# A mixture-of-experts layer on one Trainium2 core: expert results added to totals in memory instead of stored by slot and gathered by token

## The chip, the core and the metric

The kernel runs on one core of one Trainium2 chip. The metric is the device time of the whole program in microseconds (us), lower is better. The engines are named as the profile names them: PE (TensorE, matrix multiply), DVE (VectorE), ACT (ScalarE), POOL (GpSimd) and SP (SyncE). SP and POOL also issue the transfers (DMAs): SP the plain ones for inputs, weights and outputs, POOL those of this change, among them the ones whose rows are chosen by a list of indices.

## What is computed

512 tokens (8 sequences of 64) of 512 numbers each pass through three residual layers: attention to a context of 8 x 1601 rows, a graph-like attention among the 64 tokens of a sequence, and a mixture of 8 experts. The change is in the third, so the rest is left out here:

```python
logits = x @ router_w.T + router_b                     # 8 logits a token
topk_val, topk_idx = jax.lax.top_k(logits, 2)
weights = jax.nn.softmax(topk_val, axis=-1)            # two weights a token
h = xf @ wa.T + ba                                     # an expert: 512 -> 2 x 2048
h1, h2 = jnp.split(h, 2, axis=-1)
out = (silu(h1) * h2) @ wb.T + bb                      # -> 512
combined = (gathered * weights.reshape(-1, 2, 1)).sum(axis=1)
x = x + combined
```

`gathered` holds, for each token, the outputs of its two experts. All arithmetic is in float32.

## The kernel before

**The front, 0 to 385 us.** Tokens are handled in four tiles of 128, held in `xs[t]`. Generators for the steps of a tile (`queries`, `scores`, `average`, `mix`, `attend`, `route`) are interleaved by a hand-made clock, and TensorE's order is pinned with explicit dependencies (`in_line`). After the first tile's `average`, `clear` writes zeros to the DRAM tensor `sorted_x` (8 x 512 rows of 512 numbers), after the second's to `sorted_y` of the same size.

**Routing.** `route(t)` normalizes a tile into `xr`, computes logits, picks two experts for each token and counts, for each expert, how many earlier tokens chose it. That gives each token two places, `expert * 512 + position`, kept in `place`, and two weights, kept in `weight`. Two indirect DMAs on POOL (L583) scatter the rows of `xr` to these places of `sorted_x`. The experts' output bias, weighted, is added to `xs[t]` at once (L603), so that `xs[t]` is what the experts' outputs are still to be added to.

**The experts, 385 to 880 us.** The number of tokens of each expert is loaded into registers of PE, ACT, DVE and POOL. Each expert's rows are handled in blocks of up to 128, by `level(e, j, xT)`: where at most 64 rows of a block are left, the arm `narrow` runs, otherwise `dense`, and after a dense block, where more than 128 rows are left, the next level. All arms exist in the program; every engine branches for itself. An arm that an engine doesn't take has instructions of its own, which make up for the semaphore counts of the arm.

- `dense` takes transposed rows `xT`. For each of 16 chunks of the hidden layer it computes `h` (L769, a PSUM tile with two buffers), ACT applies silu (L777), DVE adds the bias and multiplies (L780). It then transposes the next block's rows (`turn`, L740) and accumulates the output `o` over the 16 chunks (L791). ACT copies `o` to `y` (L795) and POOL stores `y` to `sorted_y` (L796).
- `narrow` holds 64 rows, with the two halves of the 128 partitions working on different columns. Four steps of matmuls (L812, L824), silu (L832), a multiply on DVE (L833), transposes (L836) and a copy (L837) give the hidden layer; `on` is accumulated (L843), copied by ACT (L851) and stored in two pieces (L854).
- Rows are loaded from `sorted_x` by `load_rows_of` (L725) on POOL, with dependencies on all eight scatters. The first block of an expert is loaded two experts ahead, a further block at the start of the dense block before it.
- Weights come in panels of 1 MB over SP (L153), 12 for each expert.

With this input the blocks are, from the trace: expert 0 dense; 1 and 2 narrow; 3 and 4 dense; 5 narrow; 6 three dense and one narrow; 7 dense and narrow. That is 7 dense and 5 narrow blocks.

**The end.** For each tile and each of a token's two places an indirect DMA on POOL gathers rows of `sorted_y` (L909), DVE multiplies by the weight and adds to `xs[t]` (L915), and SP stores the tile (L918).

Of the kernel before, what the change touches and what calls it, by code (L numbers as in the profile page):

```python
# [9 lines left out]
F32 = mybir.dt.float32  # L10
AF = mybir.ActivationFunctionType
ALU = mybir.AluOpType
AX = mybir.AxisListType
PSUM = bass.MemoryType.PSUM

P = 128
# [4 lines left out]
def tile_perceiver_layer(  # L21
# [27 lines left out]
    nc = tc.nc  # L49
    B, T, D = x.shape  # L50
    S = context.shape[1]
    NT = B * T
    NTT = NT // P
# [3 lines left out]
    E = b2.shape[0]  # L57
# [7 lines left out]
    outf = out.flatten_outer_dims()  # L65

    const = ctx.enter_context(tc.tile_pool(name="const", bufs=1))
    small = ctx.enter_context(tc.tile_pool(name="small", bufs=2))
# [7 lines left out]
    xs = [const.tile([P, D], F32, name=f"xs{t}") for t in range(NTT)]  # L76
# [37 lines left out]
    for e in range(1, E):  # L114
# [7 lines left out]
        out=tri, in_=tri, pattern=[[1, P]], compare_op=ALU.is_gt, fill=0.0, base=0,  # L122
        channel_multiplier=-1,
# [6 lines left out]
        nc.gpsimd.memset(first[:, e : e + 1], float(e * NT))  # L130
    masks = const.tile([P, NTT, E], F32, name="masks")
    place = const.tile([P, NTT, 2], mybir.dt.int32, name="place")
    weight = const.tile([P, NTT, 2], F32, name="weight")
    counts = const.tile([1, E], mybir.dt.int32, name="counts")
    scatters = []

    dram = ctx.enter_context(tc.tile_pool(name="dram", bufs=1, space=bass.MemoryType.DRAM))
    sorted_x = dram.tile([E * NT, D], F32, name="sorted_x")  # L140
    sorted_y = dram.tile([E * NT, D], F32, name="sorted_y")


    NPAN = NP1 + NP2
# [11 lines left out]
    def layernorm(dst, src):  # L156
        mean, rstd = moments(src)
        nc.vector.tensor_scalar(dst, src, mean, rstd, ALU.subtract, ALU.mult)
# [14 lines left out]
    with ExitStack() as attn:  # L173
# [49 lines left out]
        def buffers(t):  # L223
            return wide if t < NTT - 1 or not cross_done else beside[0]

        def pair(t):
            return 2 if buffers(t) is wide else 1
# [39 lines left out]
        qks, qbs = {}, {}  # L267

        def queries(t):
            xn = wide.tile([P, D], F32, tag="xr", name="xn", bufs=2)  # L270
            layernorm(xn, xs[t])
            hT = turned(t, xn)
            yield 0.8
            qT = wide.tile([P, ND, P], F32, tag="vT", name="qT")
            add_bias(qT, project_T(t, wq_sb, hT), bq_sb)
            yield 0.8
            qks[t] = tok.tile([P, ND, P], F32, tag="qk", name="qk", bufs=NTT)
            nc.vector.tensor_copy(qks[t], project_T(t, wk_sb, qT))
            qb_ps = bank(t, [P, 1], "few", "qb_ps")
            for k in range(ND):  # L280
                matmul(qb_ps, qT[:, k, :], bk_sb[:, k : k + 1], start=(k == 0), stop=(k == ND - 1))
            qbs[t] = small.tile([P, 1], F32, tag="qb", name="qb", bufs=NTT)
            nc.vector.tensor_scalar(qbs[t], qb_ps, SCALE, None, ALU.mult)
# [134 lines left out]

        avgs = {}

        def clear(rows_of, avg):

            zeros = wide.tile([P, D], F32, tag="y", name="zeros")
            nc.vector.tensor_tensor(zeros, avg, avg, ALU.is_lt)
            for e in range(E):
                nc.gpsimd.dma_start(
                    out=rows_of[e * NT : (e + 1) * NT, :].rearrange("(j p) d -> p j d", p=P),
                    in_=zeros.unsqueeze(1).to_broadcast([P, NTT, D]),
                )

        def mix(t):

# [91 lines left out]


        def route(t):
            xn = buffers(t).tile([P, D], F32, tag="xr", name="xr", bufs=pair(t))
            layernorm(xn, xs[t])
            yield 7.5
            rT = turned(t, xn)  # L530
            yield 1.0
# [22 lines left out]
            for u in range(t + 1):  # L554
# [13 lines left out]
            nc.vector.reciprocal(norm, norm)  # L568
            nc.vector.tensor_scalar(told[:, 1, :], told[:, 1, :], norm, None, ALU.mult)
            nc.vector.tensor_tensor(told[:, 0, :], pos, first, ALU.add)  # L570
            both = small.tile([P, 2, 2, E], F32, tag="both", name="both", bufs=2)
            nc.vector.tensor_tensor(
                both,
                picks.unsqueeze(2).to_broadcast([P, 2, 2, E]),
                told.unsqueeze(1).to_broadcast([P, 2, 2, E]),
                ALU.mult,
            )
            found = small.tile([P, 2, 2], F32, tag="found", name="found")
            nc.vector.tensor_reduce(found, both, AX.X, ALU.add)
            nc.vector.tensor_copy(place[:, t, :], found[:, :, 0])  # L580
            nc.vector.tensor_copy(weight[:, t, :], found[:, :, 1])
            for c in range(2):
                scatter = nc.gpsimd.indirect_dma_start(  # L583
                    out=sorted_x,
                    out_offset=bass.IndirectOffsetOnAxis(ap=place[:, t, c : c + 1], axis=0),
                    in_=xn,
                    in_offset=None,
                )

                for other in scatters:  # L590
                    tc.declare_no_dep(scatter.ins, other.ins, reason="no two tokens share a row")
                scatters.append(scatter)
# [8 lines left out]
            mm = bank(t, [P, D], "", "mm")  # L601
            matmul(mm, gT, b2_sb, start=True, stop=True)
            nc.vector.tensor_tensor(xs[t], mm, xs[t], ALU.add)  # L603

        def hidden_bias_rows():
            for i in range(b1.shape[1] // P):
# [36 lines left out]
        def crossing(first):  # L643

            for t in range(NTT):
                yield from first if t == 0 else scores(t, 1)
                yield from average(t)
                averaged.append(t)
                if t < 2:
                    clear([sorted_x, sorted_y][t], avgs[t])  # L650
                for j in range(1, NSB):
                    if t + 1 < NTT:
                        load_context(t + 1, j)
                if t + 2 < NTT:
                    load_context(t + 2, 0)
            cross.close()
            early.append(ctx.enter_context(tc.tile_pool(name="early", bufs=EARLY, side="right")))
            beside.append(attn.enter_context(tc.tile_pool(name="beside", bufs=1, side="right")))
            cross_done.append(True)
            for n in range(EARLY):  # L660
                load_panel(n)
            probs.append(clear_probs(beside[0]))
# [46 lines left out]
    with ExitStack() as ffn:  # L709
# [9 lines left out]
        NC2 = NC1 // NP2  # L719
        NB = NT // P  # L720
        engines = [mybir.EngineType.PE, mybir.EngineType.Activation, mybir.EngineType.DVE, mybir.EngineType.Pool]
        def load_rows_of(e, j):
            r = rows.tile([P, D], F32, tag="r", name="r")
            at = e * NT + j * P
            read = nc.gpsimd.dma_start(out=r, in_=sorted_x[at : at + P, :])  # L725
            for scatter in scatters:
                tc.add_manual_dep(
                    read.ins,
                    scatter.ins.name,
                    mybir.DependencyInfo(  # L730
                        mybir.DependencyClass.Sync, mybir.DependencyReason.DATA
                    ),
                    reason="rows of any tile",
                )
            return r

        def turn(r, tag, after=None):
            tr = banks.tile([P, ND, P], F32, tag="t" + tag[0] + tag[-1], name="t")
# [19 lines left out]
        def dense(e, j, xT):  # L758

            r = load_rows_of(e, j + 1) if j + 1 < NB else None  # L760
            g = gpool.tile([P, NC1, P], F32, tag="g", name="g", bufs=1)
            for n in range(NC1):
                w = panels[e * NPAN + n // PC].rearrange(
# [28 lines left out]
                    o, g[:, n, :], w2_chunk(e, n), start=(n == 0), stop=(n == NC1 - 1)  # L792
                )
            y = gpool.tile([P, D], F32, tag="y", name="y")
            nc.scalar.copy(y, o)  # L795
            nc.gpsimd.dma_start(out=sorted_y[e * NT + j * P : e * NT + (j + 1) * P, :], in_=y)  # L796
            return ahead

        def narrow(e, j, xT):


            s = P // 2
            G = P // s
            M = NP1 // G
            W = D // G
            gT = gpool.tile([P, M, PC, P], F32, tag="gT", name="gT", bufs=1)
            for m in range(M):
                h = banks.tile([P, 2, PC, P], F32, tag="hn", name="hn", bufs=2)
# [39 lines left out]
                        stop=(n == NC1 - 1),  # L848
                    )
            y = gpool.tile([P, W], F32, tag="yn", name="yn")  # L850
            nc.scalar.copy(y, o)  # L851
            at = e * NT + j * P
            for q in range(G):
                nc.gpsimd.dma_start(  # L854
                    out=sorted_y[at : at + s, q * W : (q + 1) * W], in_=y[q * s : (q + 1) * s, :]
                )

# [43 lines left out]
            tc.no_sync_barrier()  # L903
            level(e, 0, turned_rows[e])

        for t in range(NTT):
            for c in range(2):
                y = rows.tile([P, D], F32, tag="r", name="back")
                nc.gpsimd.indirect_dma_start(  # L909
                    out=y,  # L910
                    out_offset=None,
                    in_=sorted_y,
                    in_offset=bass.IndirectOffsetOnAxis(ap=place[:, t, c : c + 1], axis=0),
                )
                nc.vector.scalar_tensor_tensor(  # L915
                    xs[t], y, weight[:, t, c : c + 1], xs[t], ALU.mult, ALU.add
                )
            nc.sync.dma_start(out=outf[t * P : (t + 1) * P, :], in_=xs[t])  # L918


# [65 lines left out]
```

## Time and profile before

| what | before |
|---|---|
| median of 3 runs | 905.05 us (903.5 to 906.7) |
| the profiled execution | 905.28 us, span 903.5 us |
| PE busy | 771.2 us (85% of the span) |
| DVE, ACT, POOL busy | 225.9, 159.6, 66.9 us |
| mean clock granted to TensorE | 0.932 |
| bytes moved by DMA | 165.99 MB |
| `sorted_x` clears, issue to landing | 19.1 us median of 8, 1 MB each |
| scatters to `sorted_x` | 3.4 us median of 8 |
| loads of rows `r` | 6.6 us median of 15, 256 KB each |
| stores of `y`; of `yn` | 6.8 us (7 of 256 KB); 5.4 us (10 of 64 KB) |
| gathers from `sorted_y` | 4.0 us median of 8 |

A row of the order of time reads: start and duration in us, engine, line, operation, what is written and what is read, how many were merged, and in brackets the engine's idle time before it and what ended it. Registers, branches, semaphores and the issue of a DMA are not counted as busy. A releaser is inferred: where the one named had long been done, it was another. Times of a DMA are from its issue to its landing.

### The profile page before, as it was taken

What the parts mean: (1) busy time and instruction counts of PE and PEld (TensorE: products, weight loads), DVE (VectorE), ACT (ScalarE), POOL (GpSimd) and SP (SyncE); (2) the same over time, 40 slices, a digit from 0 to 9 for tenths busy, and PEclk for the clock granted to TensorE, in tenths of its full rate; (3) what the DMA queues carried; (4) which work ended last, traced back from release to release, by engine and by line L of the source; (5) the groups of instructions that cost most, each with busy time, mean ns of one, the idle gap of its engine ahead of it and who ended that gap; (6) DMA issues with size and microseconds to landing.
All of it is one profiled execution on the core that took longest, in us unless ns stands there. A gap on an engine that the chain in (4) does not pass through costs nothing. (4 is left out here: it accounts for less than half of the span.)

```text
span 903.5 us, 11522 instructions
## 1 busy us (share of the span) xinstructions
PE 771.2 (85%) x4794; PEld 517.8 (57%) x4794; DVE 225.9 (25%) x514; ACT 159.6 (18%) x324; POOL 66.9 (7%) x114
## 2 busy tenths in 40 slices
PE   3997997997999874399998896998899999969980
PEld 3883544444454442297454875945878786559450
DVE  2322265255342464111111110201111111101012
ACT  1123144034132123021110111100111110012000
POOL 5100200300000000100000000000000000000003
PEclk9998998999899997589999898999899999979995
DMA  9930970790420821900899957749940000062004
GB/s 304 363 135 1 366 298 0 266 415 7 151 71 1 332 88 57 396 15 2 324 403 417 403 206 302 294 155 419 408 181 24 3 24 1 1 266 93 12 5 142
DMA packets 40315, 165.99 MB, mean 184 GB/s; under 512 B 3552, under 2 KB 3568, under 8 KB 27936
## 3 DMA queue, kind: packets, MB, share of 16 engines
q1 hardware_dynamic: 31968, 136.34, 38.9%
q0 software_dynamic: 8256, 28.42, 8.3%
q8 instruction: 59, 0.97, 0.4%
q14 instruction: 32, 0.26, 0.1%
HBM read 142.34 MB, written 22.41 MB: 182 GB/s over the span
## 5 line engine op out<-in xcount | busy, mean ns | idle before, releaser
L769 PE MATMUL h<-x,panel 128*128 128x128 f32 x1024 | 124.6, 288 | 22.1 <-PEq L868 21.4
L769 PEld LDWEIGHTS h<-x,panel 128*128 128x128 f32 x1024 | 123.4, 204 | 23.9 <-issue 22.6
L780 DVE SCALAR_TENSOR_TENSOR g<-h,b_sb,g 128x128 f32<-128x128 f32 x112 | 39.3, 351 | 232.3 <-ACT g L777 232.3
L791 PE MATMUL o<-panel,g 128*128 128x512 f32 x224 | 97.3, 592 | 0.0
L791 PEld LDWEIGHTS o<-panel,g 128*128 128x128 f32 x224 | 42.1, 190 | 50.2 <-issue 50.2
L777 ACT ACTIVATE g<-h,b_sb 128x128 f32<-128x128 f32 x112 | 41.1, 367 | 150.3 <-PE h L769 150.2
L201 PEld LDWEIGHTS ctr<-ident,c 128*128 128x128 f32 x384 | 43.1, 145 | 40.6 <-DVE cT L333 13.3
L201 PE MATMUL ctr<-ident,c 128*128 128x128 f32 x384 | 54.4, 286 | 13.1 <-DMA c<-in_context_dram 11.5
L769 PEld LDWEIGHTS h<-xT,panel 128*128 128x128 f32 x512 | 57.3, 192 | 2.8 <-issue 2.8
L769 PE MATMUL h<-xT,panel 128*128 128x128 f32 x512 | 57.6, 276 | 1.2 <-ACTq L868 0.6
L205 PE MATMUL sc_ps<-cT,qk 128*64 128x512 f32 (+1 forms) x256 | 54.4, 524 | 4.9 <-ACT sc L326 4.9
L333 DVE COPY cT<-ctr 128x512 f32<-128x512 f32 (+1 forms) x52 | 34.8, 670 | 61.6 <-PE ctr L201 61.2
L812 PE MATMUL hn<-panel,x 128*64 128x512 f32 x192 | 49.3, 605 | 0.0
L331 ACT COPY cT<-ctr 128x512 f32<-128x512 f32 (+1 forms) x52 | 29.6, 570 | 111.2 <-PE ctr L201 111.2
L205 PE MATMUL av<-c,pT 128*64 128x512 f32 x192 | 48.4, 642 | 0.0
L843 PE MATMUL on<-panel,gT 128*64 128x256 f32 x320 | 38.6, 381 | 0.0
L833 DVE TENSOR_TENSOR gn<-hn,gn 128x256 f32<-128x256 f32 x20 | 8.5, 425 | 103.3 <-ACT gn L832 97.7
L205 PEld LDWEIGHTS mm<-hT,w 128*128 128x128 f32 x256 | 29.2, 192 | 8.8 <-DVE hT L237 8.8
L205 PE MATMUL mm<-hT,w 128*128 128x128 f32 x256 | 30.7, 278 | 4.0 <-DVE hT L237 4.0
L812 PE MATMUL hn<-panel,xT 128*64 128x512 f32 x128 | 32.2, 596 | 0.0
L769 PE MATMUL h<-xd,panel 128*128 128x128 f32 x256 | 31.3, 288 | 0.8 <-DVE xd L751 0.8
L843 PEld LDWEIGHTS on<-panel,gT 128*64 128x64 f32 x320 | 24.5, 137 | 12.9 <-issue 0.8
(175 smaller groups left out, 703.2 us busy)
## 6 DMA issues: line engine op xcount, KB each, us to landing
panel<-in_w_dram SPq DMA_DIRECT2D x96, 1024.0 KB, 15.6
c<-in_context_dram SPq DMA_DIRECT2D x24, 1024.0 KB, 10.9
sorted_x<-zeros POOLq DMA_DIRECT2D x8, 1024.0 KB, 19.1
sorted_y<-zeros POOLq DMA_DIRECT2D x8, 1024.0 KB, 18.9
r<-sorted_x POOLq DMA_DIRECT2D x15, 256.0 KB, 6.6
sorted_y<-y POOLq DMA_DIRECT2D x7, 256.0 KB, 6.8
cl<-in_context_dram SPq DMA_DIRECT2D x8, 130.0 KB
xs<-in_x_dram SPq DMA_DIRECT2D x4, 256.0 KB, 8.4
```

Of the source, the lines that this page charges most:

```text
L201: in_line(nc.tensor.transpose(out, in_, identity))
L205: in_line(nc.tensor.matmul(out, lhsT, rhs, **flags))
L331: nc.scalar.copy(dst, tr)
L333: nc.vector.tensor_copy(dst, tr)
L769: last = nc.tensor.matmul(h[:, half, :], w[:, k, half, (n % PC) * P : (n % PC + 1) * P], xT[:, k, :], start=(k == 0), stop=(k == ND - 1),)
L777: nc.scalar.activation(g[:, n, :], h[:, 0, :], AF.Silu, bias=b1_sb[:, col : col + 1])
L780: nc.vector.scalar_tensor_tensor(g[:, n, :], h[:, 1, :], b1_sb[:, col + NC1 : col + NC1 + 1], g[:, n, :], ALU.add, ALU.mult,)
L791: nc.tensor.matmul(o, g[:, n, :], w2_chunk(e, n), start=(n == 0), stop=(n == NC1 - 1))
L812: nc.tensor.matmul(h[q * s : (q + 1) * s].rearrange("p h c d -> p (h c d)"), xT[:, k, :s], w[:, k, :], start=(k == 0), stop=(k == ND - 1),)
L833: nc.vector.tensor_tensor(gn, h[:, 1], gn, ALU.mult)
L843: nc.tensor.matmul(o[q * s : (q + 1) * s, :], gT[:, m, c, i * s : (i + 1) * s], w2_chunk(e, n)[:, q * W : (q + 1) * W], start=(n == 0), st ...
```

## The change

Results no longer go by slot to `sorted_y`. Two tensors of totals in DRAM, one for each half of the 512 columns, take their place.

- Each row of `sorted_x` gets 9 more numbers (521 in place of 512, `WIDE`): the token's number, counted from 1, and its weight for each of the 8 experts (0 where it is not chosen). The token's number is written by POOL, the weights by DVE, into the same tile `row` that is scattered. `clear` zeroes `sorted_x` only, and 128 spare rows at the end of each total.
- After the bias is added, `route` writes `xs[t]` to the totals, in two halves: two more DMAs on POOL for each tile.
- Each block loads its 9 numbers for each row (`load_shares`, on POOL; a narrow block once for each half of the partitions) and turns them on DVE, in three small instructions, into the row of the totals for each partition. An empty slot has the number 0, and is sent to a spare row of its own.
- DVE, not ACT, takes `o` out of PSUM, and multiplies by the weight. Two indirect DMAs that add (`add_to_total`) take the place of the store.
- At the end SP copies the two totals to the output, from DRAM to DRAM. The gathers, the multiply-adds and the stores of the tiles are gone.

The core of the diff:

```diff
-    sorted_x = dram.tile([E * NT, D], F32, name="sorted_x")
-    sorted_y = dram.tile([E * NT, D], F32, name="sorted_y")
+    WIDE = D + 1 + E
+    sorted_x = dram.tile([E * NT, WIDE], F32, name="sorted_x")
+    total = [dram.tile([1 + NT + P, D // 2], F32, name=f"total{h}") for h in range(2)]
...
+            zeros = wide.tile([P, WIDE], F32, tag="xr", name="zeros", bufs=2)
...
+            for h in range(2):
+                nc.gpsimd.dma_start(out=total[h][1 + NT :, :], in_=zeros[:, : D // 2])
...
+            nc.gpsimd.tensor_scalar(row[:, D : D + 1], number, float(t * P), None, ALU.add)
...
-            nc.vector.tensor_copy(weight[:, t, :], found[:, :, 1])
+            nc.vector.tensor_copy(row[:, D + 1 :], told[:, 1, :])
...
             nc.vector.tensor_tensor(xs[t], mm, xs[t], ALU.add)
+            for h in range(2):
+                nc.gpsimd.dma_start(
+                    out=total[h][1 + t * P : 1 + (t + 1) * P, :],
+                    in_=xs[t][:, h * D // 2 : (h + 1) * D // 2],
+                )
...
-                if t < 2:
-                    clear([sorted_x, sorted_y][t], avgs[t])
+                if t == 0:
+                    clear(avgs[t])
...
+        def load_shares(e, j, s):
+            shares = rows.tile([P, 1 + E], F32, tag="shares", name="shares", bufs=2)
+            for q in range(P // s):
+                read_sorted(shares[q * s : (q + 1) * s, :], e * NT + j * P, s, D, WIDE)
+            to = rows.tile([P, 1], mybir.dt.int32, tag="to", name="to", bufs=2)
+            row = rows.tile([P, 1], F32, tag="row", name="row", bufs=2)
+            nc.vector.tensor_scalar(row, shares[:, 0:1], 0.0, beyond, ALU.is_equal, ALU.mult)
+            nc.vector.tensor_tensor(row, row, shares[:, 0:1], ALU.add)
+            nc.vector.tensor_copy(to, row)
+            return to, shares[:, 1 + e : 2 + e]
+
+        def add_to_total(h, y, to):
+            nc.gpsimd.indirect_dma_start(
+                out=total[h],
+                out_offset=bass.IndirectOffsetOnAxis(ap=to, axis=0),
+                in_=y,
+                in_offset=None,
+                compute_op=ALU.add,
+            )
...
             r = load_rows_of(e, j + 1) if j + 1 < NB else None
+            to, weight = load_shares(e, j, P)
             g = gpool.tile([P, NC1, P], F32, tag="g", name="g", bufs=1)
...
-            nc.scalar.copy(y, o)
-            nc.gpsimd.dma_start(out=sorted_y[e * NT + j * P : e * NT + (j + 1) * P, :], in_=y)
+            nc.vector.tensor_scalar(y, o, weight, None, ALU.mult)
+            for h in range(2):
+                add_to_total(h, y[:, h * D // 2 : (h + 1) * D // 2], to)
...
+            to, weight = load_shares(e, j, s)
             gT = gpool.tile([P, M, PC, P], F32, tag="gT", name="gT", bufs=1)
...
-            nc.scalar.copy(y, o)
+            nc.vector.tensor_scalar(y, o, weight, None, ALU.mult)
             for q in range(G):
-                nc.gpsimd.dma_start(
-                    out=sorted_y[at : at + s, q * W : (q + 1) * W], in_=y[q * s : (q + 1) * s, :]
-                )
+                add_to_total(q, y[q * s : (q + 1) * s, :], to[:s])
...
-        for t in range(NTT):
-            for c in range(2):
-                y = rows.tile([P, D], F32, tag="r", name="back")
-                nc.gpsimd.indirect_dma_start(
...
-            nc.sync.dma_start(out=outf[t * P : (t + 1) * P, :], in_=xs[t])
+        for h in range(2):
+            nc.sync.dma_start(out=outf[:, h * D // 2 : (h + 1) * D // 2], in_=total[h][1 : 1 + NT, :])
```

`read_sorted` is the body of the old `load_rows_of`, with the columns as arguments; `load_rows_of` now reads columns 0 to 511 with it.

More of the change, by code (lines that the diff above doesn't have):

```diff
@@ L132, in tile_perceiver_layer @@
     place = const.tile([P, NTT, 2], mybir.dt.int32, name="place")
-    weight = const.tile([P, NTT, 2], F32, name="weight")
     counts = const.tile([1, E], mybir.dt.int32, name="counts")
     scatters = []
+    number = const.tile([P, 1], F32, name="number")
+    nc.gpsimd.iota(
+        number, pattern=[[0, 1]], base=1, channel_multiplier=1, allow_small_or_imprecise_dtypes=True
+    )
+    beyond = const.tile([P, 1], F32, name="beyond")
+    nc.gpsimd.tensor_scalar(beyond, number, float(NT), None, ALU.add)
     dram = ctx.enter_context(tc.tile_pool(name="dram", bufs=1, space=bass.MemoryType.DRAM))
-    sorted_x = dram.tile([E * NT, D], F32, name="sorted_x")
-    sorted_y = dram.tile([E * NT, D], F32, name="sorted_y")
+    WIDE = D + 1 + E
+    sorted_x = dram.tile([E * NT, WIDE], F32, name="sorted_x")
+    total = [dram.tile([1 + NT + P, D // 2], F32, name=f"total{h}") for h in range(2)]
     NPAN = NP1 + NP2
@@ L269, in queries @@
         def queries(t):
-            xn = wide.tile([P, D], F32, tag="xr", name="xn", bufs=2)
+            xn = wide.tile([P, WIDE], F32, tag="xr", name="xn", bufs=2)[:, :D]
             layernorm(xn, xs[t])
@@ L419, in tile_perceiver_layer, with clear @@
         avgs = {}
-        def clear(rows_of, avg):
-            zeros = wide.tile([P, D], F32, tag="y", name="zeros")
-            nc.vector.tensor_tensor(zeros, avg, avg, ALU.is_lt)
+        def clear(avg):
+            zeros = wide.tile([P, WIDE], F32, tag="xr", name="zeros", bufs=2)
+            nc.vector.tensor_tensor(zeros[:, :D], avg, avg, ALU.is_lt)
+            nc.vector.tensor_copy(zeros[:, D:], zeros[:, : 1 + E])
             for e in range(E):
                 nc.gpsimd.dma_start(
-                    out=rows_of[e * NT : (e + 1) * NT, :].rearrange("(j p) d -> p j d", p=P),
-                    in_=zeros.unsqueeze(1).to_broadcast([P, NTT, D]),
-                )
+                    out=sorted_x[e * NT : (e + 1) * NT, :].rearrange("(j p) d -> p j d", p=P),
+                    in_=zeros.unsqueeze(1).to_broadcast([P, NTT, WIDE]),
+                )
+            for h in range(2):
+                nc.gpsimd.dma_start(out=total[h][1 + NT :, :], in_=zeros[:, : D // 2])
         def mix(t):
@@ L526, in route @@
         def route(t):
-            xn = buffers(t).tile([P, D], F32, tag="xr", name="xr", bufs=pair(t))
+            row = buffers(t).tile([P, WIDE], F32, tag="xr", name="xr", bufs=pair(t))
+            xn = row[:, :D]
             layernorm(xn, xs[t])
+            nc.gpsimd.tensor_scalar(row[:, D : D + 1], number, float(t * P), None, ALU.add)
             yield 7.5
@@ L570, in route @@
             nc.vector.tensor_tensor(told[:, 0, :], pos, first, ALU.add)
-            both = small.tile([P, 2, 2, E], F32, tag="both", name="both", bufs=2)
             nc.vector.tensor_tensor(
[L573 to L576, printed above, removed]
-            )
-            found = small.tile([P, 2, 2], F32, tag="found", name="found")
-            nc.vector.tensor_reduce(found, both, AX.X, ALU.add)
-            nc.vector.tensor_copy(place[:, t, :], found[:, :, 0])
-            nc.vector.tensor_copy(weight[:, t, :], found[:, :, 1])
+                picks, picks, told[:, 0, :].unsqueeze(1).to_broadcast([P, 2, E]), ALU.mult
+            )
+            found = small.tile([P, 2], F32, tag="found", name="found")
+            nc.vector.tensor_reduce(found, picks, AX.X, ALU.add)
+            nc.vector.tensor_copy(place[:, t, :], found)
+            nc.vector.tensor_copy(row[:, D + 1 :], told[:, 1, :])
             for c in range(2):
@@ L585, in route @@
                     out_offset=bass.IndirectOffsetOnAxis(ap=place[:, t, c : c + 1], axis=0),
-                    in_=xn,
+                    in_=row,
                     in_offset=None,
@@ L721, in tile_perceiver_layer, with read_sorted @@
         engines = [mybir.EngineType.PE, mybir.EngineType.Activation, mybir.EngineType.DVE, mybir.EngineType.Pool]
[L722 to L725, printed above, removed]
+        def read_sorted(out, at, n, first, end):
+            read = nc.gpsimd.dma_start(out=out, in_=sorted_x[at : at + n, first:end])
             for scatter in scatters:
@@ L734, in load_rows_of @@
                 )
-            return r
+        def load_rows_of(e, j):
+            r = rows.tile([P, D], F32, tag="r", name="r")
+            read_sorted(r, e * NT + j * P, P, 0, D)
+            return r
+        def load_shares(e, j, s):
[15 more added lines that the diff above has]
+                compute_op=ALU.add,
+            )
         def turn(r, tag, after=None):
@@ L850, in narrow @@
             y = gpool.tile([P, W], F32, tag="yn", name="yn")
-            nc.scalar.copy(y, o)
-            at = e * NT + j * P
+            nc.vector.tensor_scalar(y, o, weight, None, ALU.mult)
             for q in range(G):
-                nc.gpsimd.dma_start(
-                    out=sorted_y[at : at + s, q * W : (q + 1) * W], in_=y[q * s : (q + 1) * s, :]
-                )
+                add_to_total(q, y[q * s : (q + 1) * s, :], to[:s])
         def arm(cond, label):
@@ L904, in tile_perceiver_layer @@
             level(e, 0, turned_rows[e])
-        for t in range(NTT):
-            for c in range(2):
-                y = rows.tile([P, D], F32, tag="r", name="back")
[L909 to L917, printed above, removed]
-            nc.sync.dma_start(out=outf[t * P : (t + 1) * P, :], in_=xs[t])
+        for h in range(2):
+            nc.sync.dma_start(out=outf[:, h * D // 2 : (h + 1) * D // 2], in_=total[h][1 : 1 + NT, :])
 def _layout(v):
```

## The prediction

> **What bounds the kernel now.** I read the page first, then busy time and clock by stage, then POOL's order of time in the expert stages with the landing times of its loads, and last the final 25 us. From the page:
>
> ```profile
> span 903.5 us, 11522 instructions
> PE 771.2 (85%) x4794; PEld 517.8 (57%) x4794; DVE 225.9 (25%) x514; ACT 159.6 (18%) x324; POOL 66.9 (7%) x114
> L780 DVE SCALAR_TENSOR_TENSOR g<-h,b_sb,g 128x128 f32<-128x128 f32 x112 | 39.3, 351 | 232.3 <-ACT g L777 232.3
> ```
>
> TensorE (PE) is the bound. VectorE (DVE) has room, but each chunk of a dense block needs one L780 on DVE before its PSUM buffer `h` is free, and `h` has two buffers: DVE costs nothing while on time, and once it is late TensorE stops two chunks later. The order of time of expert 4's dense block, POOL first:
>
> ```profile
> 547.46 0.55 POOL L796 DMA_DIRECT2D sorted_y<-y  x1 [43.06 <-ACTq L868]
> 557.12 0.54 POOL L725 DMA_DIRECT2D r<-sorted_x  x1 [9.11 <-DMA r<-sorted_x]
> 559.17 0.54 POOL L725 DMA_DIRECT2D r<-sorted_x  x1 [1.51 <-DMA r<-sorted_x]
> ...
> 797.53 1.06 POOL L854 DMA_DIRECT2D sorted_y<-yn  x2 [68.34 <-ACTq L873]
> 800.46 0.57 POOL L796 DMA_DIRECT2D sorted_y<-y  x1 [1.87 <-DMA r<-sorted_x]
> ```
>
> ```profile
> 554.12 16.10 PE L769 MATMUL h<-x,panel 128*128 128x128 f32 x120 [6.67 <-PEq L868]
> ```
>
> ```profile
> 562.21 0.37 ACT L777 ACTIVATE g<-h,b_sb 128x128 f32<-128x128 f32 x1 [1.70 <-PE h L769]
> 564.00 0.37 ACT L777 ACTIVATE g<-h,b_sb 128x128 f32<-128x128 f32 x1 [1.42 <-PE h L769]
> ```
>
> POOL is idle 9.11 us between storing expert 3's rows and its next load, since it goes past an arm not taken only when the store has landed (median 6.8 us for L796, 5.4 us for L854). TensorE needs none of that now: rows are loaded a block ahead. But POOL reaches the dense block's own load (559.17) 5 us after TensorE started there. The last two POOL rows show that a queue keeps its order: expert 6's `y` was ready at 769.8 us and stored at 800.46, because another store stood in front, waiting. All loads of rows, issue to landing, in us:
>
> ```profile
> DMA to landing us min/median/max: 2.9/6.6/8.2
> ```
>
> In the two quiet blocks (682 to 735 us, DMA share 0.05) the median is 3.3. A third thing is the clock. After a gap TensorE runs slowly; here expert 4's first 3.9 us, after a gap of 6.67 (columns: PE, weight load, DVE, ACT, POOL busy, then clock, DMA share, GB/s):
>
> ```profile
> 554.10:558.00 3.90, 3.88 (x18) 3.90 (x19) 0.00 (x0) 0.00 (x0) 0.54 (x1) 0.50 1.01 420
> ```
>
> The end, behind the last matmul:
>
> ```profile
> 878.78 0.37 ACT L851 COPY yn<-on 128x256 f32<-128x256 f32 x1 [7.26 <-PE on L843]
> 879.45 1.06 POOL L854 DMA_DIRECT2D sorted_y<-yn  x2 [26.66 <-ACTq L873]
> 884.85 1.01 POOL L909 DMA_INDIRECT back<-sorted_y,place  x1 [4.34 <-issue]
> ...
> 898.40 1.54 DVE L915 SCALAR_TENSOR_TENSOR xs<-back,weight,xs 128x512 f32<-128x512 f32 x2 [0.92 <-DMA back<-sorted_y,place]
> ```
>
> 24 us without a matmul: store, wait, eight gathers, eight multiply-adds, four stores.
>
> **The sum's base.** The profiled execution took 905.28 us (span 903.5, 1.8 around it); the runs' median is 905.05, so the two are taken as one.
>
> **Removed and cheap parts.** The clear of `sorted_y` (eight DMAs, 6.0 us of POOL at 175) goes; in 95 to 215 us TensorE waits for no context load, so this is worth 0. The new rows of totals (eight DMAs of 128 KB and two spare ones, about 0.55 us each on POOL) lie where POOL idles; the last two follow the last token scatters (369.94), and the loads behind them wait 8.03 us for those scatters anyway. If that cover failed: +1.1. Marking and weights in `route` exchange one small DVE instruction for another and add one on POOL: 0. The eviction of `y` moves from ACT (585 ns) to DVE (nearest row: the PSUM copy L751, 690 ns); the next block's first chunks hide it, and at the very end it costs the same as ACT's 0.37.
>
> Rows become 2,084 bytes. No row of the trace has that size; with 2,048 bytes a clear lands in 19.1 us and the slowest token scatter in 8.1. The Trainium skill, "DMA: Bandwidth & Descriptors", section "How a descriptor splits into AXI transactions", splits a row into 256-byte transactions with a leftover and an extra one for an unaligned start: 9 or 10 in place of 8. By the row the change costs 0 at the front; by the rule, estimated, up to a quarter of 8.1 us. I take +1 (0 to +2): the first loads wait for that scatter, TensorE for them. The clear has 35 us of slack before the first scatter.
>
> **The end.** The last block's two adds replace its two stores. By the gathers' rows, 1.0 us each with 0.30 between: the second starts at 880.75. How long an add takes to land no row shows. Bounds: below, the plain store of this place, 1.9; above, twice the slowest token scatter, 16 (each row is read as well as written). I take 4.2, the token scatter's median 3.4 and a little: 885. Passing the arm not taken, as before from 882.0 to 883.6, and the issue: 887. The copy moves 1 MB in two DMAs; nearest rows are an unhindered 1 MB weight load, 5.5 us, and an output store, 2.8: I take 5.5 (2.8 to 11, memory being at both ends). With the 1.5 us that followed the last landing before: 894. So -9 (-4 to -12), were all else equal.
>
> **The new wait.** Every block now loads its tokens and shares (`load_shares`) on POOL and, on DVE, turns them into row numbers at once: three small instructions whose first waits for that load. The block needs the result only at its end, but DVE runs in order, so the L780s or L833s behind them wait too, and with them TensorE. On POOL itself 17 share loads (7 dense blocks, 5 narrow ones with two) and 24 adds stand in place of 17 stores: about 9 + 24 in place of 9 us, spread over 495 us in which it idles; what they delay is POOL's next loads, counted below. SP waits for the adds only with its two copies, and nothing is queued behind those. Where among DVE's instructions the three stand, the trace of before can't show. Bounds: in front of all, or behind so many that the load is in. They come first in the source, but an instruction whose input is not ready can be passed; I take them behind the second chunk or the third of a dense block, and behind the first of a narrow one.
>
> Arrival at expert 4 as the example: POOL at 559.17, later by 1.3 since two adds (1.0 each, 0.3 between) start where one store did and POOL waits for the second; +0.55 to issue the row load that stands in front; +6.6 to land (r's median; the small load follows r's rows on one queue): 567.6; +0.9 for the three (0.16 each) and the L780 behind: 568.5. Behind the second chunk, TensorE can finish the third, and would start the fourth at 562.21: it stops 6.3 us. In the same way, with 3.3 us to land in the quiet blocks and two share loads in a narrow block: expert 3 (503.86, needed 508.9) 4.2; expert 6's three dense blocks (638.87, 685.29, 728.66) 3.6, 3.8, 3.4; expert 7 (806.41, needed 813.7) 2.8. Narrow blocks, needed at the second transpose L836: expert 1 (444.30, needed 448.2) 6.1; expert 2 (474.55, 476.8) 7.6; expert 5 (610.18, 611.9) 8.3. Expert 0 (load issued at 384.62, before TensorE's start), 6's narrow block (POOL idle long before) and 7's last: 0. Sum 46.1. Behind the third chunk each dense block stops 1.8 less: 35.3.
>
> Gaps of 3.8 us and more are followed by the half clock about 4 us after they begin, for 6.8 us (493.4: clock 0.5 from 497.3 to 504.1; 547.4: from 551.9 to 558.7); what of that falls on running matmuls costs half. Five stops are that long: (6.8 - (stop - 4.2))/2 gives 11 us, or 9 in the second case. So 57 or 44; I take 50 between them.
>
> 905.3 + 50 - 9 + 1 = 947.
>
> A rule against that size: the same page, section "Anatomy of one DMA — SWDGE (gpsimd) path", fits 2.0 us plus bytes/436e3 to such a DMA: 2.0 for the 4.6 KB of shares. The row says 6.6 for r beside the panels, 3.3 without. By the rule the stops shrink by 4.6 (1.3) us to 15 in all, none long enough for the half clock, and the sum is 912. The trace's own rows decide: the load shares a queue with r, whose fastest of 15 took 2.9.
>
> **Rivals.** (1) Faster: the three stand so far back that the shares are in. From behind about the eighth dense chunk and the third narrow one, no block stops and only the end counts: 905.3 - 9 + 1 = 897. For it: nothing needs the result early. Against: they are first in the source. With the copy at its upper bound this becomes no change. (2) Short stops, by the page's 2 us: 912. Against: the landing rows. (3) Adds that land slowly. POOL passes the next expert's arm only when they have landed; from about 13 us instead of 6.8 the six stops at the experts' borders grow by 6 each: 947 + 36 = 983. No row excludes it. The three in front of all chunks gives 71 of stops and about 975.
>
> **How the numbers follow.** The stops: 0.70, own range 920 to 975. Rival 2: 0.06. Rival 3 and dearer: 0.08. Rival 1: 0.13 faster, 0.03 no change. 0.3% (2.7 us) is about what a measurement of this kernel can tell from no change. The range leaves out rival 1 and no more: 906 to 985. Faster 0.13, same 0.03, slower 0.84.
>
> **What would show it.** Right: TensorE idle in front of L769 and L836 (new lines) ended by DVE, some 3 to 8 us a block, DVE idle ended by the load of `shares`, POOL's loads 1 to 2 us later than before, a last matmul near 930, and an end of 15 us in place of 24. Wrong: no idle time of DVE on `shares`; or an end as long as before, which sinks the -9; or front stages that moved by more than 2 us.

## The result, and the profile after

| what | before | after |
|---|---|---|
| median of 4 runs | 905.45 us | 1021.1 us (1017.0 to 1027.6) |
| ratio, with its 95% interval | | 1.128 (1.124 to 1.132) |
| span of the profiled execution | 903.5 us | 1015.3 us |
| mean clock granted to TensorE | 0.932 | 0.892 |
| first turn of expert 0 (L740; after, L781) starts at | 384.84 us | 383.54 us |
| last matmul ends at about | 878.8 us | 1001.6 us |
| from there to the end | 24.7 us | 13.7 us |
| bytes moved by DMA | 165.99 MB | 157.10 MB |

The direction was forecast, the size was not: +116 us, where +42 was forecast, and outside the range. All of the loss lies between the first turn and the last matmul: 494 us before, 618 after. TensorE in this stretch, before and after (columns: length, then busy PE, weight load, DVE, ACT, POOL, then clock, DMA share, GB/s):

```profile
384.84:878.80 493.96, 458.20 (x3076) 337.91 (x3076) 65.96 (x167) 64.64 (x152) 14.40 (x27) 0.96 0.45 181
```

```profile
383.54:1001.60 618.06, 480.16 (x3076) 352.35 (x3076) 78.00 (x214) 59.14 (x140) 51.56 (x51) 0.88 0.38 145
```

The same 3076 matmuls take it 22.0 us longer, at a lower mean clock (0.88, 0.96 before), and it is idle 102.1 us longer. From the page of the changed kernel (a group's busy time in us and mean in ns, then the idle time before it, and after each arrow how much of that this releaser ended; PEq and DVEq are the engine's own sequencer):

```profile
span 1015.3 us, 11588 instructions
PE 793.3 (78%) x4794; PEld 532.7 (52%) x4794; DVE 231.4 (23%) x554; ACT 153.9 (15%) x312; POOL 98.6 (10%) x138
...
L811 PE MATMUL h<-x,panel 128*128 128x128 f32 x1024 | 132.3, 298 | 71.7 <-DVE g L822 51.3
...
L811 PE MATMUL h<-xT,panel 128*128 128x128 f32 x512 | 62.5, 288 | 11.6 <-DVE g L822 10.4
...
L770 POOL DMA_INDIRECT total<-y,to x14 | 22.7, 1625 | 343.9 <-DVE y L837 146.2
...
L880 PE MATMUL tn<-ident,gn 128*128 128x128 f32 x40 | 9.5, 322 | 42.2 <-DVE gn L877 41.5
L764 DVE TENSOR_SCALAR row<-shares,beyond 128x1 f32<-128x1 f32 x12 | 2.6, 214 | 174.9 <-DMA shares<-sorted_x 174.9
```

TensorE waits for DVE's `g` for 51.3 and 10.4 us in dense blocks and for `gn` for 41.5 us in narrow ones: 103.2 us of stops in all. The first and the last of these groups in the kernel before wait 0.7 us for `g`, and 0.7 us in all for the transposes:

```profile
L769 PE MATMUL h<-x,panel 128*128 128x128 f32 x1024 | 124.6, 288 | 22.1 <-PEq L868 21.4 <-DVE g L780 0.7
L836 PE MATMUL tn<-ident,gn 128*128 128x128 f32 x40 | 8.8, 301 | 0.7
```

DVE's own wait is in the last row of the changed kernel's page above: all 12 times that the first of the three small instructions (L764) came, it waited for the shares, 174.9 us together. It is not long itself (2.6 us); what counts is who stands behind it. Expert 4's dense block in the order of time, DVE first, then TensorE, then POOL:

```profile
616.57 0.21 DVE L764 TENSOR_SCALAR row<-shares,beyond 128x1 f32<-128x1 f32 x1 [24.60 <-DMA shares<-sorted_x]
616.81 0.16 DVE L765 TENSOR_TENSOR row<-row,shares 128x1 f32<-128x1 f32 x1
617.18 0.15 DVE L766 CAST to<-row 128x1 int32<-128x1 f32 x1 [0.21 <-DVE row L765]
617.25 0.60 DVE L822 SCALAR_TENSOR_TENSOR g<-h,b_sb,g 128x128 f32<-128x128 f32 x2
```

```profile
597.57 5.56 PE L811 MATMUL h<-x,panel 128*128 128x128 f32 x32 [6.33 <-PEq L909]
617.65 27.21 PE L811 MATMUL h<-x,panel 128*128 128x128 f32 x224 [14.52 <-DVE g L822]
```

```profile
606.86 0.61 POOL L740 DMA_DIRECT2D r<-sorted_x  x1 [11.66 <-DMA total<-y,to]
609.22 0.57 POOL L740 DMA_DIRECT2D r<-sorted_x  x1 [1.75 <-DMA total<-y,to]
609.82 0.54 POOL L740 DMA_DIRECT2D shares<-sorted_x  x1
```

The three stand in front of every L822 of the block. TensorE does exactly two chunks (32 matmuls, both buffers of `h`), stops for 14.52 us, and goes on 0.4 us after DVE's first L822. POOL asked for the shares 12.3 us after TensorE had begun the block, since it first waited 11.66 us for expert 3's adds to land; 6.6 us later the shares were in.

The end is as forecast. The last block's result, its two adds and the two copies:

```profile
1001.61 0.48 DVE L895 TENSOR_SCALAR yn<-on,shares 128x256 f32<-128x256 f32 x1 [5.76 <-PE on L887]
1002.39 1.51 POOL L770 DMA_INDIRECT total<-yn,to  x1 [25.75 <-DVEq L914]
1004.21 1.44 POOL L770 DMA_INDIRECT total<-yn,to  x1 [0.30 <-issue]
1009.03 1.26 SPq L948 DMA_DIRECT2D out_dram<-total  x2
```

### The profile page after: what moved, and what is told of

It reads as the page before. It is cut to its first block, busy times and chain, and to the rows that moved or that the text cites. A ratio compares the mean times of both kernels' runs of the same rounds, so it can differ in the third digit from the quotient of the medians.

```text
span 1015.3 us, 11588 instructions
## 1 busy us (share of the span) xinstructions
PE 793.3 (78%) x4794; PEld 532.7 (52%) x4794; DVE 231.4 (23%) x554; ACT 153.9 (15%) x312; POOL 98.6 (10%) x138
## 2 busy tenths in 40 slices
DMA packets 40944, 157.10 MB, mean 155 GB/s; under 512 B 4080, under 2 KB 7552, under 8 KB 28560
## 5 line engine op out<-in xcount | busy, mean ns | idle before, releaser
L811 PE MATMUL h<-x,panel 128*128 128x128 f32 x1024 | 132.3, 298 | 71.7 <-DVE g L822 51.3
L811 PEld LDWEIGHTS h<-x,panel 128*128 128x128 f32 x1024 | 130.9, 213 | 73.5 <-DVE g L822 52.1
L833 PE MATMUL o<-panel,g 128*128 128x512 f32 x224 | 97.3, 592 | 0.0
L822 DVE SCALAR_TENSOR_TENSOR g<-h,b_sb,g 128x128 f32<-128x128 f32 x112 | 38.7, 350 | 162.3 <-ACT g L819 159.4
L811 PE MATMUL h<-xT,panel 128*128 128x128 f32 x512 | 62.5, 288 | 11.6 <-DVE g L822 10.4
L811 PEld LDWEIGHTS h<-xT,panel 128*128 128x128 f32 x512 | 61.8, 204 | 13.6 <-DVE g L822 10.7
L833 PEld LDWEIGHTS o<-panel,g 128*128 128x128 f32 x224 | 42.0, 190 | 50.2 <-issue 50.2
L856 PE MATMUL hn<-panel,x 128*64 128x512 f32 x192 | 55.5, 676 | 3.2 <-DVEq L919 3.1
L770 POOL DMA_INDIRECT total<-y,to x14 | 22.7, 1625 | 343.9 <-DVE y L837 146.2
L880 PE MATMUL tn<-ident,gn 128*128 128x128 f32 x40 | 9.5, 322 | 42.2 <-DVE gn L877 41.5
L764 DVE TENSOR_SCALAR row<-shares,beyond 128x1 f32<-128x1 f32 x12 | 2.6, 214 | 174.9 <-DMA shares<-sorted_x 174.9
L856 PEld LDWEIGHTS hn<-panel,x 128*64 128x64 f32 x192 | 20.7, 156 | 23.7 <-issue 18.8
```

What stands on the lines that cost most here:

```text
L770: nc.gpsimd.indirect_dma_start(out=total[h], out_offset=bass.IndirectOffsetOnAxis(ap=to, axis=0), in_=y, in_offset=None, compute_op=ALU.add,)
L811: last = nc.tensor.matmul(h[:, half, :], w[:, k, half, (n % PC) * P : (n % PC + 1) * P], xT[:, k, :], start=(k == 0), stop=(k == ND - 1),)
L822: nc.vector.scalar_tensor_tensor(g[:, n, :], h[:, 1, :], b1_sb[:, col + NC1 : col + NC1 + 1], g[:, n, :], ALU.add, ALU.mult,)
L833: nc.tensor.matmul(o, g[:, n, :], w2_chunk(e, n), start=(n == 0), stop=(n == NC1 - 1))
L856: nc.tensor.matmul(h[q * s : (q + 1) * s].rearrange("p h c d -> p (h c d)"), xT[:, k, :s], w[:, k, :], start=(k == 0), stop=(k == ND - 1),)
L880: nc.tensor.transpose(tr[:, c, :], gn[:, c, :], ident)
```

## The experiments

The theory after the result: the three instructions in front of each block make the loss, by the in-order wait on DVE; the adds only move the arrival of the shares; the half clock follows the stops. Rival A: the adds are the cost themselves, wherever the three stand. Rival B: it is the scaling of `y` on DVE.

**1. The three behind the last chunk.** One explicit dependency (an order within DVE's program, no wait) holds them behind the last L822 of a dense block, or the last multiply of a narrow one. All else stays. `places_of` is these three instructions, `shares` what they read, `mixed` the instruction that they are held behind:

```diff
-            to, weight = load_shares(e, j, P)
+            shares, weight = load_shares(e, j, P)
...
-                nc.vector.scalar_tensor_tensor(
+                mixed = nc.vector.scalar_tensor_tensor(
...
+                if n == NC1 - 1:
+                    to = places_of(shares, mixed)
```

> The three DVE instructions that turn the shares into row numbers stand behind the last L822 of a dense block and the last L877 of a narrow one; loads, adds and the scaling of y on DVE stay. Theory (in front of the block they make DVE wait, and TensorE with it): the 103 us of stops and the half clock behind them (about 15) go, the 11 us gained at the end and about 6 us lost at the turns stay: 895 to 905 us, TensorE idle behind DVE g or gn under 5 us in all. Rival A (the adds, their 1.6 us on POOL and their slow landing, are the cost wherever the three stand): 990 or more. Rival B (the scaling of y on DVE): 1000 or more.

Measured: 900.55 us, 0.997 (0.995 to 0.999) of the kernel before. Groups of its profile:

```profile
L822 PE MATMUL h<-x,panel 128*128 128x128 f32 x1024 | 123.2, 285 | 23.0 <-PEq L924 21.6 <-DVE g L833 1.4
L895 PE MATMUL tn<-ident,gn 128*128 128x128 f32 x40 | 8.7, 300 | 0.7
L767 DVE TENSOR_SCALAR row<-shares,beyond 128x1 f32<-128x1 f32 x12 | 2.4, 204 | 0.0
```

With the same loads and the same adds, the three wait 0.0 us and TensorE 1.4 us for `g`. Moving three instructions that take half a microsecond together is worth 120 us. Rivals A and B fall.

**2. The three where the prediction had put them**, behind the second chunk of a dense block and the first step of a narrow one; against experiment 1:

```diff
-                if n == NC1 - 1:
+                if n == 1:
                     to = places_of(shares, mixed)
...
-                if m == M - 1:
+                if m == 0:
                     to = places_of(shares, mixed)
```

> The three stand where the prediction put them: behind the second chunk of a dense block and behind the first step of a narrow one. The prediction's own sum for this place: stops of 46.1 us, 11 of half clock: 905 + 57 - 9 + 1 = 954 us. Theory now (place and arrival were both mis-sized): each stop of the changed kernel shrinks by two chunks (3.6 us) or one narrow step (4.2 us) and no more, to about 66 us in all: 975 to 985 us. If only the place was wrong: 954, and stops of about 46 us.

Measured: 982.87 us, 1.086 (1.083 to 1.090).

```profile
L822 PE MATMUL h<-x,panel 128*128 128x128 f32 x1024 | 134.7, 300 | 57.1 <-DVE g L833 36.8 <-PEq L924 20.1
L822 PE MATMUL h<-xT,panel 128*128 128x128 f32 x512 | 60.9, 283 | 6.4 <-DVE g L833 4.9 <-PEq L924 1.4
...
L895 PE MATMUL tn<-ident,gn 128*128 128x128 f32 x40 | 9.5, 323 | 27.3 <-DVE gn L890 26.8
```

The stops sum to 36.8 + 4.9 + 26.8 = 68.5 us, so the place alone is worth 103.2 - 68.5 = 34.7. The prediction had worked out 46.1 for this very place, but it had miscounted. Expert 4's dense block:

```profile
589.07 5.56 PE L822 MATMUL h<-x,panel 128*128 128x128 f32 x32 [6.49 <-PEq L924]
595.08 3.84 PE L822 MATMUL h<-x,panel 128*128 128x128 f32 x32 [0.45 <-DVE g L833]
610.09 23.18 PE L822 MATMUL h<-x,panel 128*128 128x128 f32 x192 [11.18 <-DVE g L833]
```

TensorE does four chunks (64 matmuls) before it stops, not three: once DVE has done two, both buffers of `h` are free again. By the prediction's own arrivals that is 1.8 us less in each of its six dense blocks, 35.3 us in place of 46.1. So the later arrival of the shares, 68.5 against 35.3, is worth about 33.

**3. The wait alone, in the kernel before.** Wider rows, the loads of shares and the three in front are added to the kernel before; stores, gathers and `y` on ACT stay. `load_shares` here issues the loads and the three; nothing uses what they give:

```diff
+            load_shares(e, j, P)
             g = gpool.tile([P, NC1, P], F32, tag="g", name="g", bufs=1)
```

> The kernel before, with its stores, gathers and y on ACT, and of the change only the wider rows, the loads of shares and the three DVE instructions in front of each block; their result is used by nothing. Theory: the wait alone makes most of the loss, from earlier arrivals than with adds (stores land in 5 to 7 us): stops of about 70 us, 10 to 15 of half clock, no gain at the end: 980 to 995 us. Rival A (the adds are the cost): under 920 us.

Measured: 994.17 us, 1.098 (1.095 to 1.102).

```profile
L795 PE MATMUL h<-x,panel 128*128 128x128 f32 x1024 | 133.7, 300 | 59.8 <-DVE g L806 38.6 <-PEq L895 21.2
L795 PE MATMUL h<-xT,panel 128*128 128x128 f32 x512 | 61.2, 284 | 7.6 <-DVE g L806 6.4 <-ACTq L895 0.6 <-PEq L895 0.6
L863 PE MATMUL tn<-ident,gn 128*128 128x128 f32 x40 | 9.5, 322 | 34.4 <-DVE gn L860 33.7
```

78.7 us of stops with no add in the kernel. The wait is enough for most of the loss (+90 us of +116).

**4. Indirect stores that write, in place of those that add.** The sums of the two experts and of the residual are left out, so this kernel serves the timing alone.

```diff
                 in_=y,
                 in_offset=None,
-                compute_op=ALU.add,
```

> The changed kernel with indirect stores that write in place of those that add, so the sums of two experts and of the residual are left out. Theory: POOL takes about 1.0 us for each in place of 1.6 and they land about as the stores did, so the six stops at the experts' borders shrink by about 3.5 us each: 995 to 1005 us. Rival A (reading and adding at memory is the cost): under 940 us. If the accumulation costs nothing: 1018 to 1024 us.

Measured: 992.78 us, 1.099 (1.093 to 1.105); slightly more saved than expected.

```profile
L810 PE MATMUL h<-x,panel 128*128 128x128 f32 x1024 | 134.0, 300 | 58.8 <-DVE g L821 39.0 <-PEq L908 19.8
L810 PE MATMUL h<-xT,panel 128*128 128x128 f32 x512 | 62.0, 286 | 9.4 <-DVE g L821 8.1 <-PEq L908 1.2
L770 POOL DMA_INDIRECT total<-y,to x14 | 14.1, 1006 | 343.6 <-DVE y L836 146.4 <-DVEq L908 96.8 <-DVEq L918 51.3
L879 PE MATMUL tn<-ident,gn 128*128 128x128 f32 x40 | 9.5, 323 | 26.6 <-DVE gn L876 25.9
```

The stops are 73.0 us; the adding costs 103.2 - 73.0 = 30. Each instruction takes POOL 1.0 us in place of 1.63, and expert 3's two land in 6.6 to 6.8 us, where those that add took 9.1 to 11.0. Expert 4 then reads:

```profile
592.07 5.37 PE L810 MATMUL h<-x,panel 128*128 128x128 f32 x32 [6.43 <-PEq L908]
606.85 27.92 PE L810 MATMUL h<-x,panel 128*128 128x128 f32 x224 [9.40 <-DVE g L821]
```

```profile
596.18 0.58 POOL L740 DMA_DIRECT2D r<-sorted_x  x1 [7.84 <-PE h L810]
```

POOL's first load comes 4.1 us after TensorE's start of the block, and in the changed kernel 9.3 (606.86 - 597.57). The 5.2 us of difference are the 5.1 by which the stop is longer there. The adds cost time only through this arrival: experiment 1 has them all, and 1.4 us of waits for `g`.

**5. `y` scaled on ACT, the three late.** In dense and narrow blocks alike, against experiment 1:

```diff
-            nc.vector.tensor_scalar(y, o, weight, None, ALU.mult)
+            nc.scalar.mul(y, o, weight)
```

> The three late as in the first experiment, and y scaled on ACT (its copy out of PSUM takes the weight as a factor) in place of DVE. Theory (the first experiment's waits of 3.1 and 2.9 us before the turn's next matmul at experts 1 and 5, and 1 us for o, come from y in front of the copy of turned rows on DVE): these go back to about 0.9 and 0, some 5 us less: 892 to 898 us. Rival (y on DVE is hidden): 899 to 902, no change to the first experiment.

Measured: 895.46 us, 0.990 (0.987 to 0.993). The passage from expert 0 to expert 1 on DVE, in the changed kernel and then in this one:

```profile
430.98 0.75 DVE L837 TENSOR_SCALAR y<-o,shares 128x512 f32<-128x512 f32 x1 [12.82 <-PE o L833]
435.42 0.69 DVE L792 COPY x<-t 128x512 f32<-128x512 f32 x1 [3.68 <-DVEq L919]
```

```profile
434.00 0.69 DVE L803 COPY x<-t 128x512 f32<-128x512 f32 x1 [14.22 <-PE t L792]
```

Between `y` and the copy of expert 1's turned rows DVE goes through the arms that it doesn't take, 3.68 us. Without `y` it waits only for the turn (`t`) when the copy comes: it must have passed them while TensorE was still accumulating `o`. TensorE's second turn there waits 3.61 us in the changed kernel and 0.84 here, as before. The prediction had put this move at 0.

**6 and 7. A table of all shares.** The 9 numbers of all rows are loaded once, in three DMAs before expert 0 (`load_table`), and turned into row numbers once, between experts 0 and 1 (`all_places`; expert 0 turns its own late in its block); the blocks load nothing but rows. With `y` on DVE (6) and on ACT (7).

```diff
+        table = load_table()
...
+            if e == 1:
+                tos.append(all_places())
```

> The shares of all rows are loaded once, in three DMAs on POOL ahead of expert 0, and turned into row numbers once on DVE between experts 0 and 1 (for expert 0 late in its block); the blocks load none. y stays on DVE. Theory (17 loads of shares in POOL's queue cost nothing once nobody waits for them early): the same as the first experiment, 897 to 904 us, with up to 2 us more at expert 1. Rival (the loads delay POOL's rows or the adds, and through them TensorE): 5 us or more below the first experiment.

> The table of the shares and y scaled on ACT together. Theory: as the late three with y on ACT, within 2 us: 891 to 898 us, faster than before by about 1%. If the shares' loads cost time of their own: 3 us or more below that kernel.

Measured: 898.77 us, 0.994 (0.992 to 0.996), and 894.26 us, 0.991 (0.987 to 0.994). Experiments 5 and 7 overlap: the 17 loads of shares cost nothing that can be measured once nobody waits for them early. Moving `y` to ACT gives 4.5 us here, close to the 5.1 from experiment 1 to 5, though the intervals of 6 and 7 overlap a little. Experiments 5 and 7 both beat the kernel before by about 1%; which of them is the better one can't be told.

**8. Shares ahead of the rows on POOL's queue.** In a dense block the 4.6 KB of shares are asked for before the next 256 KB of rows.

```diff
-            r = load_rows_of(e, j + 1) if j + 1 < NB else None
             to, weight = load_shares(e, j, P)
+            r = load_rows_of(e, j + 1) if j + 1 < NB else None
```

> The changed kernel with the loads of a dense block exchanged: its 4.6 KB of shares in front of the next rows (256 KB) on POOL. Theory (panels in flight set the landing of about 6.6 us, whatever the size): the shares still land in about 6.5 us, they are only issued 0.6 us earlier, so the seven dense stops shrink by 0.6 each: 1014 to 1020 us. Rival (the shares land late because the rows stand in front of them in the queue): they land in 2 to 4 us, dense stops shrink by 3 to 5 us each in the border blocks: 990 to 1005 us.

Measured: 1011.08 us, 1.118 (1.114 to 1.121), just under the range of the theory and above that of its rival. The landing of the shares of experts 1 to 5; the narrow blocks among them, where nothing was exchanged, have 6.3 us and more:

```profile
DMA to landing us min/median/max: 5.2/6.4/7.2
```

In the four dense blocks beside panels (experts 3, 4, 7 and the first of 6) they now land in 5.2 to 5.4 us, where they took 6.6 to 7.2. So a large load in front costs a small one 1.3 to 1.9 us, which the theory had at nothing; the other 5 are there without it. In the quiet blocks of expert 6 of the changed kernel they land in 2.6 to 3.7. That the panels in flight make this difference is the likely reading; no run took the panels away.

## Why the prediction was wrong

Point by point, by its own steps:

- **The mechanism**, a wait on DVE in front of L780/L833 that stops TensorE two chunks later: right, and shown by experiments 1 and 3.
- **The place of the three**: failed. The prediction took them behind the second or third chunk and the first narrow step, because "an instruction whose input is not ready can be passed". Here nothing passed them: they stand in front of all. Its own bound for that was 71 us of stops, and experiments 3 and 4, where no store adds, have 78.7 and 73.0: that bound was good, the choice between the bounds was not. Against the 46.1 that it used this is worth 25 us. But 46.1 was one chunk a block too long, as experiment 2 shows; against the 35.3 that its arrivals give for this place it is worth 36, and 34.7 was measured. The miscount made the forecast better by luck. The 35.3 that it gives for the third chunk is too long by the same step.
- **The price of an add**: failed. From the gathers' row 1.0 us on POOL was taken; it is 1.63 for `y` and 1.49 for `yn`. For the landing between blocks the prediction kept the store's 6.8 us; beside panels it is 9 to 12 for `y` (median of the two 11.3 at expert 0, 10.0 at expert 3). At expert 4 POOL's loads came not 1 to 2 but 6 us later against TensorE than before (9.3 us into the block, not 3.0). Worth 30 us by experiment 4. This was rival 3 (adds that land slowly, +36), which came true together with the wrong place: 35.3 + 36 + 30 = 101 of the 103.2 us of stops.
- **The half clock**: its length failed, and so its cost, 11 us where it is about 22. Slices of 3 us (columns as above; the third number from the end is the mean clock) around the stop at expert 4, which ends at 617.65:

```profile
606.00:609.00 3.00, 0.00 (x0) 0.00 (x0) 0.00 (x0) 0.00 (x0) 0.61 (x1) 0.85 1.03 434
609.00:612.00 3.00, 0.00 (x0) 0.00 (x0) 0.00 (x0) 0.00 (x0) 1.11 (x2) 0.50 1.01 419
...
618.00:621.00 3.00, 3.00 (x15) 3.00 (x15) 0.00 (x0) 0.00 (x0) 0.00 (x0) 0.50 1.00 418
621.00:624.00 3.00, 3.00 (x26) 3.00 (x25) 0.49 (x2) 0.73 (x2) 0.00 (x0) 0.88 1.04 431
```

  The prediction let it last 6.8 us from its beginning, so that a stop of 11 us would outlast it. Here it begins 2 to 5 us into a stop, holds to the stop's end and for about 4 us of work after it: 15 matmuls in the first slice after the restart, 26 in the next. In slices of 0.5 us the full clock comes back 2.8 to 5.4 us after the restart (mean 4.3) in all nine stops of 5 us and more, so that each costs about half of that, whatever its length: some 19 us, where the prediction's rule gives 6.5 for the same nine. The 22.0 us by which TensorE is busy longer agree with that; the rest was not followed. The trace of before had a row against the 6.8 us, after its longest gap (8.33 us, TensorE starts again at 805.12):

```profile
801.00:811.20 10.20, 6.08 (x28) 6.11 (x29) 0.35 (x1) 1.65 (x2) 0.57 (x2) 0.50 0.99 407
```

  By its own threshold of 3.8 us the prediction also had six long stops, not five (expert 6's second): 3.5 us more by its rule. The Trainium skill, "TensorE: Matmul & The Clock Gate", section "Part 1: The HAM clock gate (the "warmup" mystery)", has full speed come back after some 3.4 us of sustained work, in a window that doesn't start with the work; of the nine restarts here two took less (2.8 and 3.3 us), the others up to 5.4. Nine times half of 3.4 would have been an estimate of 15.
- **`y` on DVE at nothing, hidden by the next block's chunks**: failed where the next block begins with a copy of turned rows. What the cover had to hide was not the 0.75 us of `y` alone but DVE's way through its arms. Worth 5 us from experiment 1 to 5. In the changed kernel itself it does not show in the sum, since two turns behind narrow blocks (experts 3 and 6) wait 1.04 us each, where they waited 3.81 and 3.67 before; why, no run shows.
- **The 2 us for a small DMA**, by the fit of the Trainium skill, "DMA: Bandwidth & Descriptors", section "Anatomy of one DMA — SWDGE (gpsimd) path", which the prediction refused in favour of the landing rows: rightly. Shares beside panels took 6.4 to 7.2 us, in quiet blocks 2.6 to 3.7.
- **The end, -9**: -11, right; the adds land in 3.1 us and the copies in at most 3.7, where 4.2 and 5.5 were taken.
- **The front, +1**: the first turn starts 1.3 us earlier in the profiled execution. In kernels with the same front it ranges from 382.9 (experiment 1) to 388.3 (experiment 8), with 384.8 before, so a microsecond can't be told there. The removed clear and the new rows of totals cost nothing that shows.
- **Rival 1** (faster, 897, if the three stand far back) was the right number for another kernel: experiment 1 is it, at 900.55, and with the turn's 5 us mended, experiment 5, at 895.46.

The sum with the terms measured, all from the profiled execution: 905.3 + 102 (more idle time: the stops, and the turns, which nearly cancel) + 22 (the clock) - 11 (end) - 1 (front) = 1017. The profiled execution took 1017.0 us; the median of the runs is 1021.1.

## What to carry to other kernels

Ask of every new instruction that waits for a DMA what stands behind it in its engine's order, and read the order of the program before choosing between bounds: when nothing but the order is unknown, "in front of all" is the case to price first. Put such an instruction behind the last one that the critical engine needs, with an order-only dependency; here that alone turned +12.8% into -0.3%. An engine that gets work at the end of a block also pays for the branches that it used to pass early (3.68 us of DVE at the border from expert 0 to 1).

## What the runs showed that was not expected

- An indirect DMA that adds takes POOL 1.63 us for 128 rows of 1 KB, one that writes 1.0. Beside panel loads `y` lands in 9 to 12 us against 6.4 to 7.1, in quiet blocks in 3.7 to 4.0 against 2.4 to 3.1.
- 4.6 KB and 256 KB take nearly the same time to land (median 6.4 and 6.5 us over all loads of the changed kernel); even with the 4.6 KB in front, experiment 8, they take 5.2 to 5.4 us beside panels.
